# Order and queues of the opening loads in an attention, state-space and expert layer

## The chip, the cores and the metric

The kernel runs on one core of a Trainium2 chip. The core has five engines that run their own instruction streams: TensorE (PE, with its weight loads shown apart as PEld), VectorE (DVE), ScalarE (ACT), GpSimd (POOL) and SyncE (SP), which here only issues transfers. ScalarE issues transfers too. Sixteen DMA engines move the data. The metric is device time in microseconds; the time before is the median of three runs.

## The reference

One layer of a perceiver with 256 latents of width 512 and a context of 4096 rows of width 512, all in float32:

- x = x + attention(layernorm(x), context). 16 query heads and 4 key heads of width 128. Keys and values come both from the context (4096 keys, seen by all) and from the latents themselves (causal). Queries and keys are RMS-normed per head with a learned weight; queries and the latents' own keys are turned by rotary tables.
- x = x + state-space block(layernorm(x)).
- x = x + experts(layernorm(x)): 32 experts, the best 6 for each latent, and a shared one.

What matters here is only the start of the first part: layernorm(x), the first keys of the context (context times wk_ctx), the latents' own keys and queries, and the rotary tables, which are built once from cosines and sines (rope) and the norm weights (w_bc).

## The kernel before

**Tiling and stages.** The context is worked in eight chunks of 512 rows, each of four tiles of 128 rows. Chunk 0 is handled in the opening; chunks 1 to 7 are projected between the attention's steps. The latents are two row tiles of 128. A weight of 512 x 512 is held as four quarters of 128 rows (k = 0 to 3), so a projection of one tile is four matmuls in the code (eight instructions in the trace: a float32 matmul shows as two).

**The opening loads (L86 to L104, L132 to L138).** ScalarE's queue issues nw (the norm weights on one partition, for a flag), rope, w_bc (the norm weights copied to all partitions) and kw_col. rope has rows of 512 bytes, w_bc of 1 KB, kw_col of 4 bytes; the others have rows of 2 KB. SyncE's queue issues context tile 0 (`load_ctx0(0, 1)`), the keys' weights in three pieces (`load_wkc`: quarter 0, quarter 1, quarters 2 and 3), x, context tile 1, context tiles 2 and 3, and the values' weights wvc. Behind the branch on the flag (L1601 to L1608) SyncE issues wk, the four pieces of wq, wv and the next chunks. A transfer signals its landing on one of eight semaphores that are used in turn; a later transfer that takes the same one is issued only when the earlier one has landed.

**The opening work (L465 to L512).** TensorE's stream is: the keys of context tiles 0, 1 and 2 (ps_k, L309), the eight transposes of the normed latents (lnT, L212), the values of tile 0 (ps_v, L316), the transpose of the keys of tile 0 (kTp, L291), then the latents' own keys (ps_self, L479), which read the turned latents xT, with more transposes and queries behind it.

VectorE makes what these need: the layer norm of x (statistics at L201 and L203, then `power_half` with its small operation pv at L195, then xn at L206, one for each row tile), the rotary tables (`rope_table`, eight operations at L441 and L442 that read rope and w_bc, written into the first part of oacc), four small operations on w_bc (L555 to L559), pv for the keys' norms, and the two copies of the transposes into xT (L213). The power itself runs on GpSimd (L196). Behind the second power GpSimd makes three sums of the keys' and values' weights for a later stage (`weight_sums`, L330 to L332):

```python
with tc.issue_after(normed.ins):
    weight_sums(*sums)
```

where `normed` is the layer norm's last power.

**What sets the order.** Each engine runs its instructions in the order that a scheduler wrote at build time from the code, from costs and from what each instruction needs; `issue_after` adds a wish. The order in the code is thus not the order on VectorE: the table operations stand between the layer norm's. Transfers keep the order of the code on their queue.

Of the kernel before, what the change touches and what calls it, by code (L numbers as in the profile page):

```python
# [11 lines left out]
FP = mybir.dt.float32  # L12
# [7 lines left out]
P = 128  # L20
L = 256
NT = L // P
# [8 lines left out]
HD = 128  # L31
HALF = HD // 2
# [41 lines left out]
def perceiver_layer(ctx: ExitStack, tc: tile.TileContext, a: dict, out: bass.AP):  # L74
    nc = tc.nc
    V, S, G, TE = nc.vector, nc.scalar, nc.gpsimd, nc.tensor

    early = ctx.enter_context(tc.tile_pool(name="early", bufs=1))
    const = ctx.enter_context(tc.tile_pool(name="const", bufs=1))
# [10 lines left out]
    wkc, wvc = wkv[:, 0], wkv[:, 1]  # L90
# [1 line left out]


    load_ctx0 = lambda i, n: nc.sync.dma_start(ctx0[:, i:i + n], a["ctxT"][0, :, i:i + n])
    load_wkc = lambda k, n: nc.sync.dma_start(wkc[:, k:k + n, :],
                                              a["wk_ctx"][k * P:(k + n) * P, :].rearrange("(k p) n -> p k n", p=P))
    load_ctx0(0, 1)
    load_wkc(0, 1)
    load_wkc(1, 1)
    load_wkc(2, 2)  # L100
    nc.sync.dma_start(x_sb, a["x"].rearrange("(t p) d -> p t d", p=P))
    load_ctx0(1, 1)
    load_ctx0(2, 2)
    nc.sync.dma_start(wvc, a["wv_ctx"].rearrange("(k p) n -> p k n", p=P))  # L104

    nb = const.tile([1, 2], FP, name="nb")
    V.tensor_reduce(nb, nw, AX.X, ALU.max, apply_absolute_value=True)
# [20 lines left out]
    kd = [tc.dram_tile((CK // P, NKV, HD, P), FP, name=f"kd{c}") for c in range(NC)]  # L128
    blocks_d = [tc.dram_tile((REP, HD, P), FP, name=f"qd{i}") for i in range(NT * NH // REP)]
    sums_d = [tc.dram_tile((SH, P), FP, name=f"sums{t}") for t in range(NT)]  # L130

    rope = const.tile([P, NT, 2, HALF], FP, name="rope")  # L132
    S.dma_start(rope, a["rope"].rearrange("(t p) c h -> p t c h", p=P))
    w_bc = const.tile([P, 2, HD], FP, name="w_bc")
    S.dma_start(w_bc, a["norm_ws"].partition_broadcast(P))
    qw_bc, kw_bc = w_bc[:, 0, :], w_bc[:, 1, :]
    kw_col = const.tile([P, 1], FP, name="kw_col")
    S.dma_start(kw_col, a["norm_ws"][1, :].unsqueeze(1))  # L138

    def layer(ctx, bounded):  # L140
        small = ctx.enter_context(tc.tile_pool(name="small", bufs=4))
# [1512 lines left out]
```

## Time and profile before

| what | value |
|---|---|
| median of 3 runs | 992.71 us (991.9 to 994.02) |
| the profiled execution's own time | 989.35 us |
| its span in the profile | 987.6 us |
| TensorE busy | 968.4 us (98%) |
| VectorE busy | 497.8 us (50%) |
| ScalarE busy | 386.5 us (39%) |
| GpSimd busy | 206.0 us (21%) |
| moved | 125.91 MB, mean 127 GB/s |
| landing of rope, w_bc, kw_col after issue | 4.2, 5.6, 7.3 us |
| landing of the values' weights after issue at 6.08 | 9.5 us |

The profile shows one execution. A line of the timeline has the start, the duration of the group, the engine, the line of the code, the operation, what it writes and reads, how many instructions are merged, and in brackets the idle time before it and what ended it. In a table of stretches each engine's busy time and instruction count stand in one row, and the last two columns are the busy share of the DMA engines and GB/s. An engine's idle time matters only if TensorE, which is busy nearly throughout, comes to wait for it.

### The profile page before, as it was taken

Reading aid. Unit: us, or ns where it says so; the run is one execution under the profiler, and the core shown is the slowest. Engines: PE = TensorE matmul, PEld = TensorE weight load, DVE = VectorE, ACT = ScalarE, POOL = GpSimd, SP = SyncE. Lnnn points to the kernel's source line nnn. Section 1 sums busy time; section 2 is a strip of 40 time slices with the busy share of each in tenths; the row PEclk is TensorE's granted clock in tenths of the full one; section 3 lists DMA queues with packets and bytes.
Section 4 is the critical chain, followed back from the end, with each engine's and each line's share of the span. In section 5 each row is a group of like instructions: output and inputs, shape, how many; then the busy total and the mean of one; then the engine's idle time right before and its main releaser. Section 6 shows DMA issues by size and latency. Waiting matters only on the chain.

```text
span 987.6 us, 8901 instructions
## 1 busy us (share of the span) xinstructions
PE 968.4 (98%) x2742; PEld 456.0 (46%) x2742; DVE 497.8 (50%) x999; ACT 386.5 (39%) x851; POOL 206.0 (21%) x212
## 2 busy tenths in 40 slices
PE   7999999999999999999999999999999999999996
PEld 3444444444444444444444444444465655555442
DVE  4456555454453544544535545458496766422134
ACT  3645444443443434434434444353253731222210
POOL 4443001001100200200200100000013224554533
PEclk9999999999999999999999999999999999999999
DMA  9734142222313304304204112240046452999953
GB/s 319 235 74 118 56 117 94 45 39 111 85 21 128 85 2 147 82 4 150 66 20 124 56 35 46 83 128 1 0 157 199 184 193 106 353 351 352 397 221 117
DMA packets 131580, 125.91 MB, mean 127 GB/s; under 512 B 80225, under 2 KB 99586, under 8 KB 126274
## 3 DMA queue, kind: packets, MB, share of 16 engines
q1 hardware_dynamic: 119216, 77.96, 26.2%
q0 software_dynamic: 7984, 41.16, 11.2%
q10 hardware_dynamic: 4322, 6.11, 1.7%
q8 instruction: 24, 0.39, 0.2%
q14 instruction: 34, 0.28, 0.1%
HBM read 89.02 MB, written 36.19 MB: 127 GB/s over the span
## 4 chain that ended last, share of the span: by engine, by line
PE 94%; DMA 2%; DVE 1%; ACT 1%; POOL 1%; issue 1%; SPq 0%; POOLq 0%; DVEq 0%
PE scT L567 23%; PE oT L592 23%; PE ps_kv L364 17%; PE ps_egu L218 5%; PE ps_self L218 3%; PE ps_v L218 2%; PE ps_o L790 2%; PE ps_ye L1466 2%; PE ps_xbc L218 1%; PE ps_out L984 1%; PE ps_egu L1389 1%; PE ps_k L218 1%; PE ps_sgu L218 1%; PE total L1457 1%; PE xgTp L1370 1%; PE ps_ye L1469 1%
## 5 line engine op out<-in xcount | busy, mean ns | idle before, releaser
L583 DVE TENSOR_TENSOR lacc<-lacc,prT 128x512 f32<-128x512 f32 x256 | 182.6, 714 | 239.2 <-ACT prT L573 238.5
L573 ACT ACTIVATE prT<-scT,bq,rk 128x512 f32<-128x512 f32 x256 | 198.9, 777 | 253.9 <-PE scT L567 241.8
L567 PE MATMUL scT<-qT,kT 128*128 128x512 f32 x536 | 271.7, 593 | 0.0
L592 PE MATMUL oT<-prT,v 128*128 128x512 f32 x528 | 268.3, 592 | 0.0
L567 PEld LDWEIGHTS scT<-qT,kT 128*128 128x128 f32 x536 | 101.1, 190 | 124.8 <-issue 121.9
L592 PEld LDWEIGHTS oT<-prT,v 128*128 128x128 f32 x528 | 100.2, 190 | 125.8 <-issue 115.8
L196 POOL TENSOR_TENSOR rk<-pv,mhalf 128x4 f32<-128x4 f32 x32 | 32.3, 1010 | 369.2 <-DVE pv L195 369.2
L364 PE MATMUL ps_kv<-wkv,fast 128*128 128x512 f32 x112 | 53.4, 592 | 0.0
L254 ACT ACTIVATE sq<-kraw 128x128 f32<-128x128 f32 x128 | 35.6, 278 | 45.2 <-DVE kraw L382 43.2
L364 PE MATMUL ps_kv<-wkv,ctx 128*128 128x512 f32 x112 | 52.8, 592 | 0.0
L364 PE MATMUL ps_kv<-fast,fast 128*128 128x512 f32 x112 | 52.6, 592 | 0.0
L598 DVE TENSOR_TENSOR oacc<-oT,oacc 128x512 f32<-128x512 f32 x64 | 43.6, 681 | 0.0
L364 PEld LDWEIGHTS ps_kv<-wkv,fast 128*128 128x128 f32 x112 | 21.3, 190 | 26.8 <-issue 26.8
L364 PEld LDWEIGHTS ps_kv<-fast,fast 128*128 128x128 f32 x112 | 21.3, 190 | 26.8 <-issue 21.8
L364 PEld LDWEIGHTS ps_kv<-wkv,ctx 128*128 128x128 f32 x112 | 21.3, 190 | 26.8 <-issue 23.7
L358 POOL TENSOR_TENSOR fast<-ctx 128x512 f32<-128x512 f32 x7 | 9.4, 1337 | 113.1 <-PE ps_kv L364 94.2
L382 DVE TENSOR_TENSOR kraw<-ps_kv,fast 128x256 f32<-128x256 f32 x42 | 17.9, 426 | 28.2 <-PE ps_kv L364 28.2
L1441 DVE TENSOR_TENSOR hid<-si,ps_egu 128x128 f32<-128x128 f32 x18 | 5.2, 287 | 51.2 <-ACT si L1439 51.2
L790 PE MATMUL ps_o<-wo,qT 128*128 128x512 f32 x64 | 28.8, 592 | 0.0
L218 PE MATMUL ps_self<-wq,xT 128*128 128x512 f32 x64 | 28.1, 592 | 0.0
L603 DVE RECIPROCAL lacc<-ps_l 128x512 f32<-128x512 f32 x8 | 26.8, 3348 | 0.1
L364 PE MATMUL ps_kv<-fast,ctx 128*128 128x512 f32 x56 | 26.3, 592 | 0.0
(392 smaller groups left out, 1129.3 us busy)
## 6 DMA issues: line engine op xcount, KB each, us to landing
xg<-xn SPq DMA_DIRECT2D x6, 2560.0 KB, 9.7
ctx<-in_ctxT_dram SPq DMA_DIRECT2D x7, 1024.0 KB, 5.0
kd<-tr SPq DMA_DIRECT2D x112, 64.0 KB, 2.2
kT<-kd SPq DMA_DIRECT2D x28, 256.0 KB, 2.9
ye<-y_sb ACTq DMA_DIRECT2D x22, 256.0 KB, 8.4
wq<-in_wq_dram SPq DMA_DIRECT2D x4, 1024.0 KB, 14.2
wo<-in_wo_dram SPq DMA_DIRECT2D x4, 1024.0 KB, 7.7
w_in<-in_W_inT_dram SPq DMA_DIRECT2D x4, 1024.0 KB, 5.8
```

The lines of the kernel that those rows point to most:

```text
L196: return G.tensor_tensor(dst, v[:, :n], mhalf[:, :n], ALU.pow)
L218: TE.matmul(ps, lhs(k), rhs_of(k), start=(k == 0), stop=(k == KD - 1))
L254: S.activation(sq[:, h, :], raw[:, h, :], AF.Square, accum_out=ss[:, h:h + 1])
L364: TE.matmul(ps, lhs(k), rhs(k), start=(start and k == 0), stop=(k == 1), skip_group_check=True)
L567: scored.append(TE.matmul(sc, kT[:, g, i * P:(i + 1) * P], qT[:, t, heads4(g), :].rearrange("p h q -> p (h q)"), start=True, stop=True).ins)
L573: S.activation(pr, sc, AF.Exp, bias=shift, scale=SCALE if r is None else r[:, i, g:g + 1])
L583: V.tensor_tensor(la, la, pr, ALU.add)
L592: TE.matmul(outs[g, t], v[:, i, g * HD:(g + 1) * HD], pr, start=(n == 0), stop=last)
L598: V.tensor_tensor(ov, outs.pop((g, t)), ov, ALU.add)
L603: V.reciprocal(rl, ps)
L790: TE.matmul(m["ps_o", t], aT[:, t, h, :], wo[j][:, h % 4, :], start=(h == 0), stop=(h == NH - 1))
L1466: TE.matmul(ps[i], h[:, i, :], wd[i], start=True, stop=False)
```

## The change

The first quarter of the keys' weights is issued on ScalarE's queue, behind nw, instead of SyncE's. Context tile 1 stands ahead of x on SyncE's queue. rope, w_bc and kw_col go from ScalarE's queue to the end of SyncE's opening loads, behind the values' weights. No computation is changed.

```diff
-    load_wkc = lambda k, n: nc.sync.dma_start(wkc[:, k:k + n, :],
-                                              a["wk_ctx"][k * P:(k + n) * P, :].rearrange("(k p) n -> p k n", p=P))
+    load_wkc = lambda q, k, n: q.dma_start(wkc[:, k:k + n, :],
+                                           a["wk_ctx"][k * P:(k + n) * P, :].rearrange("(k p) n -> p k n", p=P))
     load_ctx0(0, 1)
-    load_wkc(0, 1)
-    load_wkc(1, 1)
-    load_wkc(2, 2)
+    load_wkc(nc.scalar, 0, 1)
+    load_wkc(nc.sync, 1, 1)
+    load_wkc(nc.sync, 2, 2)
+    load_ctx0(1, 1)
     nc.sync.dma_start(x_sb, a["x"].rearrange("(t p) d -> p t d", p=P))
-    load_ctx0(1, 1)
     load_ctx0(2, 2)
     nc.sync.dma_start(wvc, a["wv_ctx"].rearrange("(k p) n -> p k n", p=P))
+
+    rope = const.tile([P, NT, 2, HALF], FP, name="rope")
+    nc.sync.dma_start(rope, a["rope"].rearrange("(t p) c h -> p t c h", p=P))
+    w_bc = const.tile([P, 2, HD], FP, name="w_bc")
+    nc.sync.dma_start(w_bc, a["norm_ws"].partition_broadcast(P))
+    qw_bc, kw_bc = w_bc[:, 0, :], w_bc[:, 1, :]
+    kw_col = const.tile([P, 1], FP, name="kw_col")
+    nc.sync.dma_start(kw_col, a["norm_ws"][1, :].unsqueeze(1))
...
-    rope = const.tile([P, NT, 2, HALF], FP, name="rope")
-    S.dma_start(rope, a["rope"].rearrange("(t p) c h -> p t c h", p=P))
-    w_bc = const.tile([P, 2, HD], FP, name="w_bc")
-    S.dma_start(w_bc, a["norm_ws"].partition_broadcast(P))
-    qw_bc, kw_bc = w_bc[:, 0, :], w_bc[:, 1, :]
-    kw_col = const.tile([P, 1], FP, name="kw_col")
-    S.dma_start(kw_col, a["norm_ws"][1, :].unsqueeze(1))
```

In the built program TensorE's, ScalarE's and GpSimd's instructions stand in the same order as before. On VectorE the xn of row tile 0 now stands ahead of the second row tile's pv, with more of the table operations behind the second xn:

| position | before | after |
|---|---|---|
| after the statistics of both row tiles | L203, first L441 (waits for rope and w_bc), pv, L203, L442, pv | L203, first L441 (waits for rope and w_bc), pv, L203, L442, xn of tile 0, pv |
| then | L441, L442, L441, xn of tile 0, xn of tile 1 | L441, L442, xn of tile 1 |
| then | L442, L441, L442 | L441, L442, L441, L442 |
| then | four of L555 to L559, two pv, two xT copies | the same |

## The prediction

> **What bounds the kernel now.** I read the page's first part, then the busy time by stretches, then the timeline of each engine over the opening, since the change touches only transfers that are issued there.
>
> ```profile
> PE 968.4 (98%) x2742; PEld 456.0 (46%) x2742; DVE 497.8 (50%) x999; ACT 386.5 (39%) x851; POOL 206.0 (21%) x212
> ```
>
> The stretches (first column after the window is its length, then busy PE, PEld, DVE, ACT, POOL):
>
> ```profile
> 0.00:20.00 20.00, 14.60 (x34) 6.09 (x35) 8.40 (x27) 6.76 (x23) 6.84 (x14) 1.00 0.87 303
> 20.00:100.00 80.00, 79.97 (x205) 36.13 (x204) 43.66 (x76) 45.19 (x138) 35.43 (x31) 1.00 0.56 160
> 100.00:200.00 100.00, 100.00 (x235) 44.27 (x234) 49.05 (x82) 42.33 (x84) 9.10 (x8) 1.00 0.25 72
> ```
>
> TensorE has work without a break from about 10 us to 700 us. What the opening gains or loses for TensorE therefore passes one for one to the end; what it does to any other engine counts only where TensorE comes to wait for it. TensorE's own opening (start, duration):
>
> ```profile
> 5.29 13.52 PE L218 MATMUL ps_k<-wkv,ctx 128*128 128x512 f32 x24 [5.29 <-DMA wkv<-in_wk_ctx_dram]
> ...
> 18.64 1.04 PE L212 MATMUL lnT<-ident,xn 128*128 128x128 f32 x8
> ...
> 23.39 1.02 PE L218 MATMUL ps_self<-wk,xT 128*128 128x512 f32 x2
> ```
>
> It starts when the first quarter of the keys' weights lands, and 24 instructions take 13.5 us against 24 x 0.43 = 10.3 us at the later pitch. The last line is the first product that needs xT, the turned latents. Who makes xT:
>
> ```profile
> 11.06 1.29 DVE L201 BATCH_NORM_STATS2 bn<-x_sb 128x6 f32<-128x512 f32 x2 [8.20 <-DMA x_sb<-in_x_dram]
> ...
> 12.35 0.26 DVE L441 TENSOR_TENSOR oacc<-rope,w_bc 128x128 f32<-128x128 f32 x1
> 12.53 0.15 DVE L195 TENSOR_SCALAR pv<-mv 128x1 f32<-128x1 f32 x1
> ...
> 13.52 1.16 DVE L206 TENSOR_SCALAR xn<-x_sb,mv,rs 128x512 f32<-128x512 f32 x2
> ...
> 16.02 2.16 DVE L195 TENSOR_SCALAR pv<-ss 128x4 f32<-128x4 f32 x2
> 19.28 1.29 DVE L213 COPY xT<-lnT 128x512 f32<-128x512 f32 x2 [1.09 <-PE lnT L212]
> ```
>
> and GpSimd beside it, with the three weight sums:
>
> ```profile
> 12.83 1.27 POOL L196 TENSOR_TENSOR rs<-pv,mhalf 128x1 f32<-128x1 f32 x2 [10.77 <-DVE mv L203]
> 15.69 2.40 POOL L330 TENSOR_TENSOR oacc<-wkv 128x1024 f32<-128x1024 f32 x1 [1.59 <-DMA wkv<-in_wv_ctx_dram]
> 18.17 2.37 POOL L331 TENSOR_TENSOR oacc<-wkv,oacc 128x1024 f32<-128x1024 f32 x1
> 20.62 2.40 POOL L332 TENSOR_TENSOR oacc<-wkv,oacc 128x1024 f32<-128x1024 f32 x1
> ```
>
> The reader is to see that all eight rope-table operations (L441, L442) are over before the first weight sum begins, and that the tiny pv operation at 16.02 lasted until that sum ended at 18.09. The second xT copy ends at 20.57; TensorE asks for xT at 23.39: 2.8 us of slack, and 3.4 us for the first copy.
>
> **What the Trainium skill says.** "SBUF — State Buffer", Who interferes with whom: a VectorE instruction with two SBUF inputs contends with a GpSimd instruction that reads SBUF, and whichever starts first blocks the other for its whole duration. The trace agrees. Around 59 us, VectorE first, GpSimd below:
>
> ```profile
> 58.61 0.86 DVE L455 TENSOR_TENSOR lacc<-raw,oacc 128x256 f32<-128x256 f32 x1
> 59.40 1.48 DVE L456 TENSOR_TENSOR lacc<-raw,oacc 128x256 f32<-128x256 f32 x1
> ```
>
> ```profile
> 57.47 1.73 POOL L356 TENSOR_TENSOR fast<-ctx 128x512 f32<-128x512 f32 x1
> 59.28 1.33 POOL L357 TENSOR_TENSOR fast<-fast,ctx 128x512 f32<-128x512 f32 x1
> ```
>
> Both VectorE operations take 0.42 us undisturbed (at 28.8 and 29.1 us). Each ended 0.3 us after the GpSimd operation it met: one VectorE operation slips in between two GpSimd ones, not two. "DMA: Bandwidth & Descriptors", Queues, rings and completion order: each issuing engine has one ring on each of the 16 DMA engines, and a ring is consumed in order. In this trace SyncE's loads land in the order of issue. "TensorE: Matmul & The Clock Gate", What's actually happening: the array runs at half clock until it has been busy for a window of some 3.4 us. The trace agrees: starts 0.98 to 1.0 us apart from 5.29 to 9.3, 0.43 us from about 10.3.
>
> **The change, part by part.** (1) The first weight quarter moves from SyncE's to ScalarE's queue, where it is issued after nw at about 1.4 us, as rope is now; on SyncE it is issued at 1.26. No gain in issue time is certain. It shares the DMA engines with the second quarter. Bounds: its landing at 5.2 moves to between 4.5 and 6.1. (2) The remaining quarters, context tile 1, x and the rest lose the small packets ahead of them:
>
> ```profile
> 5.50:9.00 3.50, 3.50 (x4) 0.76 (x4) 0.00 (x0) 0.00 (x0) 0.00 (x0) 1.00 0.77 230
> 9.00:12.00 3.00, 2.89 (x6) 1.18 (x6) 0.94 (x2) 0.20 (x1) 0.00 (x0) 1.00 1.04 413
> ```
>
> (the last column is GB/s). While w_bc and kw_col trickled in, the engines moved 230 GB/s, afterwards about 400: 3.5 x (1 - 230/400) = 1.5 us lost, 0.2 us more from 4 to 5.5 (337 GB/s), and 262 KB of rope and w_bc are another 0.65 us: 2.4 us for the three. So TensorE's waits inside ps_k vanish. They are small, since the half-clock phase that covers them is not shortened by data that comes sooner: four starts 0.98 apart, one of 0.81 (9.46 to 10.27), nineteen of 0.43 make 12.9 us from the start instead of 13.35. With a start between 4.5 and 6.1, lnT is asked for between 17.4 and 19.0 instead of 18.64: +0.4 to -1.2 us, I take -0.4.
>
> (3) rope, w_bc and kw_col now stand on SyncE's queue behind the values' weights. Their issue slots cost nothing: each waits for one of the first three loads to land, by about 6 us, while the values' weights are still moving, and wk's issue behind them is at 7.71 now and is used only at 23.4. But VectorE's order in the built program is: statistics, first L441, which waits for rope and w_bc, and behind it the pv of the layer norm, xn of row tile 0, pv, L441, L442, xn of tile 1, then L441, L442, L441, L442, four bq operations, two pv of the keys, and only then the two xT copies. The wait on rope and w_bc is harmless now (5.6 and 7.4 us, x lands at 11.06). When do they land after? Ahead of them are 3.67 MB; 0.39 MB move by 4 us, the rest at 400 GB/s is done at 12.2; the values' weights now land when 0.43 MB more than what is ahead of them have moved, 1.1 us, so they land at 13.3 (15.6 now). rope and w_bc follow, between 0.65 us (bytes alone) and 2.4 us (all the small-packet cost); I take 1.4. Tw = 14.7, bounds 13.9 to 15.7.
>
> From Tw, by the durations above: pv +0.18, power +0.48, xn0 +1.17, second pv behind it +1.78, second power +2.08 to +2.72. xn1 starts at +2.77, ends at +3.3 (18.0): in time for lnT. But the values' weights have landed long before, so GpSimd goes straight from the power to the weight sums: L330 from +2.7 to +5.1, before the last four two-input table operations, which now meet it. The first gets in at +5.1, L331 runs to +7.8, the second gets in, L332 runs to +10.4, then the other two, four bq and two pv (1.3 us), and the first xT copy 0.7: xT at Tw + 12.4 = 27.1. TensorE, which would ask at 23.0 to 23.4, waits: 27.1 - 23.4 = +3.7 us against now. If two operations slip through each gap, xT comes at Tw + 11.0: +2.3. Late next is everything behind ps_self in TensorE's queue, and so the end. ScalarE's and GpSimd's later work has no due date before it. Sum: between the two with most weight on the first, +3.4 us, with (1) and (2) swallowed by the wait. On the profiled execution: span 987.6 to 991.0, its own time 989.35 to 992.8. The median shown, 992.71, is 3.4 above that execution, so 996.1 on the median.
>
> **The rivals.** *No stall, loads as meant* (the other side): xT is ready by the time TensorE asks for it. It decides at Tw = 23.4 - 12.4 = 11.0 or lower, or if the table operations get past the sums. Then only parts (1) and (2) count: -0.4, at the most -1.2: 991.5 to 992.3, no measurable change. For it: the DMA engines are busy from 4 us on, so everything is a bit sooner. Against it: Tw = 11.0 would need the remaining 3.5 MB moved in the 5.9 us from 4.0 to 9.9, at 600 GB/s. *Half clock gone as well*: a start at 4.2 (-1.1), the waits gone (-0.5) and two matmuls fewer at half clock (-1.1) give -2.7 us: 990.0; against it, nothing in the change makes TensorE busy earlier than the first quarter. *Late xn alone*: L441's wait delays the layer norm but the table operations are not blocked; lnT at Tw + 3.3 = 18.0 to 19.0, 0 to +0.4: 993. *Stall that cools the array*: a wait of 3.7 us can hold a whole idle window; then some four matmuls at 0.98 add 2 us: 998.1. For it, the size of the wait; against it, the same section calls the window free-running, and a whole one has to fit into the wait.
>
> **How the numbers follow.** Stall by the blocked table operations 0.70 (of it 0.06 with a cooled array), late xn or a short stall 0.10, loads as meant 0.14, half clock gone 0.06. The stall alone runs from Tw 13.9 with two per gap (+1.5) to 15.7 with one (+4.7), 994.2 to 997.4, 2 more with cooling. The range 991.9 to 998.0 leaves out the fastest case and most of the coolest. 0.2% is 2.0 us, about what a measurement of this kernel can tell from no change (the runs shown span 2.1). Slower by more than that: most of the stall's 0.70, less its lower end, 0.64; within: 0.28; faster: 0.08.
>
> **What would show it.** First L441 at 14 to 15.5 with x's statistics done several us before; L330 starting at the end of the second power; L441 and L442 behind xn stretched from 0.28 to over 2 us; xT copies at 25 to 27; TensorE's first wait between kTp and ps_self of 2 to 4 us, the rest of the trace shifted as a whole. Wrong if L441 starts before 11, or if the four table operations end before L330 begins.

## The result and the profile after

The changed kernel takes 997.5 us (median of 5 runs, 996.68 to 998.47) against 992.71 us: 1.0051 times as long, 95% interval 1.0036 to 1.0066. Beside a second set of runs of the kernel before it was 1.0050 (1.0036 to 1.0064), 994.59 against 990.51 us. It is slower by 0.5%, some 4.8 us. The kernel before took 992.71 us in the first set of runs and 989.7 to 990.5 us in the later ones, so times are compared only within a set. The profiled execution took 996.68 us, its span is 994.9 us.

Busy time by engine, then by stretches (length, busy PE, PEld, DVE, ACT, POOL, clock, DMA share, GB/s), of the changed kernel:

```profile
PE 968.1 (97%) x2742; PEld 456.7 (46%) x2742; DVE 500.9 (50%) x999; ACT 386.2 (39%) x851; POOL 205.9 (21%) x212
```

```profile
0.00:20.00 20.00, 13.08 (x28) 5.77 (x28) 4.98 (x15) 6.27 (x21) 3.96 (x13) 1.00 0.89 308
20.00:100.00 80.00, 76.33 (x198) 34.80 (x199) 46.14 (x83) 42.26 (x134) 38.55 (x32) 1.00 0.50 140
```

TensorE was busy for 14.60 and 79.97 us of these two stretches before, and for 13.08 and 76.33 now: 1.5 and 3.6 us less, so what was lost was lost early. TensorE's timeline over the opening says where (start, duration, idle time before it):

```profile
6.58 12.64 PE L218 MATMUL ps_k<-wkv,ctx 128*128 128x512 f32 x24 [6.58 <-DMA wkv<-in_wk_ctx_dram]
19.06 0.60 PE L212 MATMUL lnT<-ident,xn 128*128 128x128 f32 x4
21.40 0.66 PE L212 MATMUL lnT<-ident,xn 128*128 128x128 f32 x4 [1.74 <-DVE xn L206]
21.89 3.60 PE L218 MATMUL ps_v<-wkv,ctx 128*128 128x512 f32 x8
...
28.18 1.13 PE L218 MATMUL ps_self<-wk,xT 128*128 128x512 f32 x2 [2.25 <-DVE xT L213]
```

Subtract the starts before from these. The first matmul is 1.3 us late (6.58 against 5.29), the first transpose 0.4 (19.06 against 18.64): the early lateness is nearly made good. Then two waits that were not there before: for the second xn, and for xT. At ps_self, the first product that reads xT, the distance is 28.18 - 23.39 = 4.79 us. VectorE and GpSimd in the same stretch:

```profile
10.30 1.29 DVE L201 BATCH_NORM_STATS2 bn<-x_sb 128x6 f32<-128x512 f32 x2 [7.43 <-DMA x_sb<-in_x_dram]
...
16.14 0.29 DVE L441 TENSOR_TENSOR oacc<-rope,w_bc 128x128 f32<-128x128 f32 x1 [4.47 <-DMA w_bc<-in_norm_ws_dram]
...
17.26 0.55 DVE L206 TENSOR_SCALAR xn<-x_sb,mv,rs 128x512 f32<-128x512 f32 x1 [0.50 <-POOL rs L196]
...
18.71 2.63 DVE L206 TENSOR_SCALAR xn<-x_sb,mv,rs 128x512 f32<-128x512 f32 x1 [0.45 <-POOL rs L196]
21.26 2.48 DVE L441 TENSOR_TENSOR oacc<-rope,w_bc 128x128 f32<-128x128 f32 x1
23.67 0.28 DVE L442 SCALAR_TENSOR_TENSOR oacc<-rope,w_bc 128x128 f32<-128x128 f32 x1
23.87 2.48 DVE L441 TENSOR_TENSOR oacc<-rope,w_bc 128x128 f32<-128x128 f32 x1
...
27.44 1.28 DVE L213 COPY xT<-lnT 128x512 f32<-128x512 f32 x2
```

```profile
17.95 0.73 POOL L196 TENSOR_TENSOR rs<-pv,mhalf 128x1 f32<-128x1 f32 x1 [0.72 <-DVE pv L195]
18.65 2.41 POOL L330 TENSOR_TENSOR oacc<-wkv 128x1024 f32<-128x1024 f32 x1
21.14 2.46 POOL L331 TENSOR_TENSOR oacc<-wkv,oacc 128x1024 f32<-128x1024 f32 x1
23.67 2.53 POOL L332 TENSOR_TENSOR oacc<-wkv,oacc 128x1024 f32<-128x1024 f32 x1
```

x's statistics are done by 11.6 us, and VectorE stands still for 4.5 us until w_bc lands. Three VectorE operations then last 2.5 us instead of 0.28 or 0.55, and each ends 0.14 to 0.28 us after the weight sum beside which it ran: one for each sum. The xT copy, which began at 19.28 before, begins at 27.44.

In this execution the distance grew once more, from 5.0 to 6.9 us at 850 to 856 us, where ScalarE waited, and TensorE behind it. The first two lines are from the changed kernel's timelines of ScalarE and TensorE there, the third from ScalarE's in its second profile (experiment 9), where the distance did not grow:

```profile
855.82 0.33 ACT L1439 ACTIVATE si<-ps_egu 128x192 f32<-128x192 f32 x1 [2.57 <-remote]
856.52 0.33 PE L1448 MATMUL hidTp<-ident,hid 128*128 128x128 f32 x1 [1.80 <-DVE hid L1441]
```

```profile
854.67 0.33 ACT L1439 ACTIVATE si<-ps_egu 128x192 f32<-128x192 f32 x1 [2.19 <-PE ps_egu L218]
```

So it is not in every execution of the changed kernel; what that event is stays open. The two spans (994.9 and 987.6 us) differ by 7.3 us, the medians by 4.8. This event is one part of the difference; another is that the profiled execution of the kernel before, at 989.35 us, was 2.5 us faster than the fastest of its five runs (991.9).

### The profile page after: what moved, and what is told of

It is laid out like the page before. It is cut to its first block, busy times and chain, and to the rows that moved or that the text cites. A ratio compares the mean times of both kernels' runs of the same rounds, so it can differ in the third digit from the quotient of the medians.

```text
span 994.9 us, 8902 instructions
## 1 busy us (share of the span) xinstructions
PE 968.1 (97%) x2742; PEld 456.7 (46%) x2742; DVE 500.9 (50%) x999; ACT 386.2 (39%) x851; POOL 205.9 (21%) x212
## 4 chain that ended last, share of the span: by engine, by line
PE 91%; DVE 2%; DMA 2%; ACT 1%; POOL 1%; issue 1%; another core or an unknown queue 1%; ACTq 0%; POOLq 0%; DVEq 0%
PE oT L592 23%; PE scT L567 23%; PE ps_kv L364 17%; PE ps_egu L218 4%; PE ps_self L218 3%; PE ps_o L790 2%; PE ps_v L218 2%; PE ps_ye L1466 2%; PE ps_xbc L218 1%; PE ps_out L984 1%; PE ps_egu L1389 1%; PE ps_sgu L218 1%; PE total L1457 1%; PE xgTp L1370 1%; DMA w_bc<-in_norm_ws_dram 1%; PE ps_ye L1469 1%
```

## The experiments

Three theories were set against each other. A: w_bc comes late, so the last table operations and GpSimd's weight sums meet, and xT comes late. B: w_bc's lateness does it alone, through the layer norm that stands behind the first table operation. C: the first weight quarter's late landing is carried to the end. VectorE's order, which the scheduler wrote anew for the changed loads, is one more candidate; experiments 3 and 7 bear on it. Ratios are to runs of the kernel before beside them, with 95% intervals; distances are starts of TensorE's instructions minus those in the profile of the kernel before that was shown at the outset.

**1. The small loads back on ScalarE's queue** (w_bc and kw_col in the same way as rope, at the same place in the code).

```diff
-    nc.sync.dma_start(rope, ...)
+    S.dma_start(rope, ...)
```

> The changed kernel with rope, w_bc and kw_col back on ScalarE's queue, behind the first weight quarter; the rest of the change stays. Theory A (late w_bc puts the last table operations against the weight sums, and xT comes late): the tables are done before the sums start, TensorE does not wait for xN or xT, the end is at +0 to +0.6 us against the kernel before, some 993.0. Rival B (w_bc's lateness by itself, through the layer norm behind the first table operation): the same, since w_bc is early. Rival C (the first quarter's late landing, 1.3 us at TensorE's start, is carried to the end): +1.3 us, 994.0, TensorE's first matmul at 6 us or later and no later catching up.

989.86 us, ratio 0.9999 (0.9991 to 1.0008). TensorE's timeline:

```profile
5.92 13.46 PE L218 MATMUL ps_k<-wkv,ctx 128*128 128x512 f32 x24 [5.92 <-DMA wkv<-in_wk_ctx_dram]
...
23.96 1.02 PE L218 MATMUL ps_self<-wk,xT 128*128 128x512 f32 x2
```

No wait is marked at ps_self. The rest of the change is no measurable loss and no gain. C's 1.3 us would be 1.0013, outside the interval. But in this profile TensorE began only 0.6 us late, and at ps_self all of that was still there; 0.6 us would be 1.0006, inside the interval. So 1.3 us at the end is excluded, a carried 0.6 is not. The edit also changed VectorE's order in the built program: all eight table operations now stood ahead of the two xn, which were done at 16.44 us, still in time.

**2. The small loads moved, and nothing else** (in the kernel before, rope, w_bc and kw_col to behind the values' weights on SyncE's queue).

```diff
+    nc.sync.dma_start(rope, ...)
-    S.dma_start(rope, ...)
```

> The kernel before with only rope, w_bc and kw_col moved behind the values' weights on SyncE's queue. Theory A: the whole loss is there with this part alone: +4.3 to +5.0 us, 997.3; TensorE starts at 4.8 to 5.3 us and waits the longer for xT. Rival C: TensorE's start at 5.3 gives 1.3 us back: +3.5 us, 996.2.

993.6 us, ratio 1.0038 (1.0026 to 1.0051). TensorE's timeline:

```profile
5.38 12.81 PE L217 MATMUL ps_k<-wkv,ctx 128*128 128x512 f32 x24 [5.38 <-DMA wkv<-in_wk_ctx_dram]
18.03 0.60 PE L211 MATMUL lnT<-ident,xn 128*128 128x128 f32 x4
21.32 0.66 PE L211 MATMUL lnT<-ident,xn 128*128 128x128 f32 x4 [2.69 <-DVE xn L205]
...
28.11 1.13 PE L217 MATMUL ps_self<-wk,xT 128*128 128x512 f32 x2 [2.26 <-DVE xT L212]
```

Within the intervals, the whole loss is here (3.9 us by the medians): ps_self at 28.11, as with the full change, though TensorE began 1.2 us earlier. The earlier start only makes the wait for xn longer (2.69 instead of 1.74). The interval of the ratio holds both A's and C's figure; the trace decides for A.

**3. The weight sums later, w_bc as late as ever.** The powers are collected in a list, and the sums are put behind that of the second key tile:

```diff
-        with tc.issue_after(normed.ins):
+        with tc.issue_after(powers[3].ins):
             weight_sums(*sums)
```

> The changed kernel with GpSimd's three weight sums put behind the power for the second key tile, so that they cannot meet the table operations; w_bc is as late as in the changed kernel (16 us). Theory A: xn of tile 1 is ready at 19.3, xT at about 22, before TensorE asks for it at 23.8; only the late start's remainder is left: +0.4 us, 993.1. Rival B (late w_bc by itself delays the layer norm): TensorE still waits 2 us or more for xn or xT: 995.5 to 997.5.

990.04 us, ratio 1.0001 (0.9992 to 1.0009). VectorE's timeline, then TensorE's:

```profile
16.18 0.29 DVE L444 TENSOR_TENSOR oacc<-rope,w_bc 128x128 f32<-128x128 f32 x1 [4.81 <-DMA w_bc<-in_norm_ws_dram]
...
18.76 0.55 DVE L209 TENSOR_SCALAR xn<-x_sb,mv,rs 128x512 f32<-128x512 f32 x1 [0.45 <-POOL rs L198]
19.22 0.28 DVE L444 TENSOR_TENSOR oacc<-rope,w_bc 128x128 f32<-128x128 f32 x1
...
20.99 1.28 DVE L216 COPY xT<-lnT 128x512 f32<-128x512 f32 x2
```

```profile
23.73 1.02 PE L221 MATMUL ps_self<-wk,xT 128*128 128x512 f32 x2
```

This decides between A and B. VectorE waits for w_bc as long as before, until 16.18 us, but every operation up to the xT copies has its short duration again, xT is copied from 20.99 instead of 27.44, and TensorE does not wait. Late w_bc alone costs nothing that can be measured. VectorE's order is here that of the changed kernel, so that order alone is not the cause either.

The stretches of this run also say something about when w_bc lands (length, busy PE, PEld, DVE, ACT, POOL, clock, DMA share, GB/s):

```profile
5.50:9.00 3.50, 2.21 (x3) 1.17 (x4) 0.00 (x0) 0.00 (x0) 0.00 (x0) 1.00 1.05 400
9.00:12.00 3.00, 3.00 (x6) 1.10 (x5) 1.37 (x3) 0.00 (x0) 0.00 (x0) 1.00 1.04 395
12.00:14.40 2.40, 2.40 (x7) 1.14 (x6) 0.00 (x0) 2.07 (x3) 0.00 (x0) 1.00 1.04 224
```

Until 12 us the loads moved at the forecast 400 GB/s, and w_bc was late all the same; the slow stretch comes after.

**4. The table operations later, loads and sums as in the change.** They, and the four small ones on w_bc, are put behind the last xT copy:

```diff
-        rope_table(tab_k, kw_bc)
-        rope_table(tab_q, qw_bc)
+        with tc.issue_after(turned.ins):
+            rope_table(tab_k, kw_bc)
+            rope_table(tab_q, qw_bc)
```

> The changed kernel with the eight table operations and the four small ones on w_bc put behind the xT copies on VectorE; loads and sums stay. Theory A: xn is ready at about 13, xT at 20.5, no wait of TensorE between the keys and the queries; +0.4 us, 993.1. Rival B: the same. Rival C: the late start costs all of its 1.3 us: 994.0.

989.71 us, ratio 1.0000 (0.9991 to 1.0008). ps_self began at 24.92 without a wait. TensorE's first matmul was as late as 7.32 us in this execution, 2.0 us late, and 1.5 us of that was still there at ps_self. The xT copies began at 21.55, a microsecond later than expected: the transposes that they copy began only at 20.17, and two small operations ahead of the copies now met the sums. VectorE's timeline, then GpSimd's:

```profile
17.20 2.00 DVE L195 TENSOR_SCALAR pv<-ss 128x4 f32<-128x4 f32 x1 [3.27 <-ACT sq L254]
19.41 2.22 DVE L195 TENSOR_SCALAR pv<-ss 128x4 f32<-128x4 f32 x1 [0.21 <-ACT sq L254]
21.55 1.27 DVE L213 COPY xT<-lnT 128x512 f32<-128x512 f32 x2
```

```profile
14.36 2.37 POOL L330 TENSOR_TENSOR oacc<-wkv 128x1024 f32<-128x1024 f32 x1 [1.01 <-DMA wkv<-in_wv_ctx_dram]
```

The last line shows when the values' weights land with the changed loads, which the changed kernel's own profile doesn't show: the sum waits for them until 14.36 us.

**5. As 4, with the first quarter on SyncE's queue again.**

```diff
-    load_wkc(nc.scalar, 0, 1)
+    load_wkc(nc.sync, 0, 1)
```

> As e4 (tables behind the xT copies), and the first weight quarter back on SyncE's queue, behind context tile 0. Theory A: TensorE starts at 5.0 to 5.3 us without the small packets in its way and never waits in the opening: -0.5 us against the kernel before, 0.9995 of its time. If the late start in e1, e3 and e4 came from the chip and not from the queue, TensorE starts at 6 us or later here too.

988.94 us against 989.75: ratio 0.9989 (0.9982 to 0.9995), the only version whose interval lies below the kernel before. TensorE began at 5.73 and did not wait. The profiled execution doesn't show a gain: its first seven matmuls ran at half pace (0.85 to 0.99 us from one start to the next, 0.43 later), and ps_self was at 23.89. This version differs from experiment 4 in the first quarter's queue alone. Their intervals overlap narrowly (0.9982 to 0.9995, 0.9991 to 1.0008), so a cost of up to about 1 us for that quarter's place on ScalarE's queue, once the stall is gone, is neither shown nor excluded.

**6. The change, with only the first quarter on SyncE's queue again** (the same edit in the changed kernel).

> The changed kernel with only the first weight quarter back on SyncE's queue. Theory A: the start moves from 6.6 to about 5.2 us, and the wait for xT swallows it: ps_self at 28.1 us, the end at +4.3 to +4.8 us, ratio 1.0045 as for the whole change. Rival C (the start is carried to the end): 1.3 us less than the whole change, +3.4 us, ratio 1.0034.

993.95 us, ratio 1.0042 (1.0026 to 1.0057). TensorE's timeline:

```profile
5.08 12.06 PE L218 MATMUL ps_k<-wkv,ctx 128*128 128x512 f32 x24 [5.08 <-DMA wkv<-in_wk_ctx_dram]
...
20.79 0.66 PE L212 MATMUL lnT<-ident,xn 128*128 128x128 f32 x4 [2.86 <-DVE xn L206]
21.29 5.29 PE L218 MATMUL ps_v<-wkv,ctx 128*128 128x512 f32 x8
...
27.57 1.12 PE L218 MATMUL ps_self<-wk,xT 128*128 128x512 f32 x2 [0.56 <-DVE xT L213]
```

A start that is 1.5 us earlier than in the changed kernel is swallowed: w_bc was 0.6 us earlier in this execution (first table operation at 15.55), and ps_self is earlier by the same 0.6. The eight ps_v took 5.29 us instead of 3.60: after the wait of 2.86 us four of the matmuls ran at half clock (the granted clock was 0.63 from 20.7 to 25 us), and even that was swallowed by the wait for xT.

**7. kw_col back on ScalarE's queue.**

```diff
-    nc.sync.dma_start(kw_col, ...)
+    S.dma_start(kw_col, ...)
```

> The changed kernel with only kw_col (rows of 4 bytes) back on ScalarE's queue; a look at when w_bc lands. If kw_col's packets, which some DMA engines reach while others still have w_bc to do, keep w_bc from landing: first table operation at 15.0 us or earlier instead of 16.1. If not: 15.8 to 16.2.

The first table operation was at 15.53 us, between the two expectations. Since it was at 15.51 to 16.18 in four runs with kw_col in place (experiments 2, 3, 6 and 9), this tells nothing about kw_col. The edit did more than move one load: VectorE's order in the built program changed too, to one nearer that of the kernel before, with both xn together at 16.65. ps_self came 11.1 us after the first table operation instead of 12.0, so in this one run the other order was worth about 1 us, and the stall was there all the same. TensorE's timeline has something else:

```profile
26.65 2.07 PE L218 MATMUL ps_self<-wk,xT 128*128 128x512 f32 x2 [2.27 <-DVE xT L213]
28.51 0.85 PE L291 MATMUL kTp<-ident,kraw 128*128 128x128 f32 x3
```

Two matmuls lasted 2.07 us instead of 1.13, and the distance went from 3.3 us at ps_self to 4.8: the array had gone back to half clock (0.59 granted from 26.6 to 30.5 us). 994.75 us, one run.

**8. w_bc from 128 different rows.**

```diff
-    nc.sync.dma_start(w_bc, a["norm_ws"].partition_broadcast(P))
+    nc.sync.dma_start(w_bc, a["rope"].rearrange("(p t) c h -> p t (c h)", t=2))
```

> The changed kernel with w_bc filled from 128 different rows of 1 KB (the rotary tables' memory) instead of one row of 1 KB read 128 times; the tables are then wrong, and nothing else is left out. If reading the same row over and over makes w_bc slow: first table operation at 15.2 us or earlier instead of 16.1, xT and the end earlier by as much. If it is the size of the packets alone: 15.8 to 16.2.

VectorE's timeline:

```profile
15.16 0.29 DVE L441 TENSOR_TENSOR oacc<-rope,w_bc 128x128 f32<-128x128 f32 x1 [3.76 <-DMA w_bc<-in_rope_dram]
```

1.0 us earlier than in the changed kernel's profile (0.35 us earlier than in any run with the single row), and ps_self 1.06 us earlier, at 27.12: 993.11 us, one run. That reading one row 128 times is slower than reading 128 rows agrees with this; one run doesn't show it, with 0.67 us between the runs that kept the single row.

**9. The change once more.** (No edit.)

> The changed kernel once more, beside the same runs of the kernel before as e10. Theory A: TensorE reaches ps_self at 28 us instead of 23.4, and this distance, 4.2 to 4.8 us, stays to the end: ratio 1.0045. The further 2 us by which the first profile of the changed kernel was late from 850 us on (ScalarE waiting there) belong to that execution: the distance at the end is again the one at ps_self. If they belong to the change, they are here again, and the distance ends near 7.

994.59 us, ratio 1.0050 (1.0036 to 1.0064). TensorE's timeline:

```profile
27.56 1.45 PE L218 MATMUL ps_self<-wk,xT 128*128 128x512 f32 x2 [2.26 <-DVE xT L213]
28.80 1.06 PE L291 MATMUL kTp<-ident,kraw 128*128 128x128 f32 x4
29.65 1.92 PE L218 MATMUL ps_self<-wk,xT 128*128 128x512 f32 x2
```

ps_self is 4.17 us late; the half clock that follows the wait (0.59 granted from 27.5 to 31.5 us) adds 1.6 us (5.7 from 31.4 us on), and after that the distance moves by no more than 0.4 us to the end. The 2 us at 850 us are not there.

**10. The kernel before, with the table operations later** (edit of experiment 4, loads as before).

> The kernel before with its own loads, and the table operations and the four small ones on w_bc behind the xT copies, as in e5. If e5's gain of 0.1% comes from the loads: no change, ratio 0.9997 to 1.0003, TensorE never waits for xT in either. If it comes from VectorE's order: ratio 0.9989 as e5.

989.65 us against 990.51, ratio 0.9994 (0.9986 to 1.0003). This lies between the two expectations: whether the 0.1% of experiment 5 comes from the loads or from VectorE's order stays open.

## Why the prediction was right, and where it was off

It foretold slower, by 3.4 us, through a stall at xT; measured were 4.8, and 997.5 us is near the top of the range given (991.9 to 998.0). The sum is of the distance at ps_self, which was 4.79 in the one profile. That the medians of the first set differ by just as much is in part chance: in the later sets the loss was 3.9 to 4.2 us by the medians (experiments 2, 6 and 9).

- **The mechanism** (part 3) holds at every link: the wait of the first L441 for w_bc (4.5 us), the sums that start as the second power ends (18.65), the stretched operations, the wait between kTp and ps_self (2.25 us, forecast 2 to 4). Experiment 2 has the loss with part 3 alone, experiment 3 has none although w_bc is as late, experiment 4 has none with the table operations out of the way.
- **The step that was off is Tw**, taken as 14.7 us with bounds of 13.9 and 15.7: it was 16.14 in the changed kernel's profile, and 15.51 to 16.18 in four repeats (experiments 2, 3, 6 and 9). Of the sum's shortfall of 1.4 us (4.8 against 3.4), this 16.14 - 14.7 = 1.4 is all. I had let the queue move 400 GB/s from 4 us on, and it moved 373 and 377 from 5.5 to 12 us in the changed kernel. That cannot be the main reason: in experiment 3 it moved 400 and 395 there, and w_bc was as late. The term that was too small is the cost of the small rows, which I had worked out from their old place, 1.4 us (at most 2.4) from 13.3 on; 16.14 is 2.8 later than that. The rate fell already from 12 us on (224 GB/s up to 14.4 in experiment 3), and the values' weights, forecast for 13.3, landed at 14.36 in experiment 4. In experiments 7 (kw_col elsewhere) and 8 (w_bc from 128 rows) the stretch from 12 to 14.4 us moved 356 and 362 GB/s, against 210 to 322 in the seven profiles with both loads as in the change; these are one run each and only suggest that both take part.
- **From Tw to xT** I had 12.4 us with one operation for each gap between the sums, 11.0 with two. To the end of the first copy it was 28.12 - 16.14 = 12.0. But the distribution was another: I let xn of tile 1 finish beside the first sum ("in time for lnT"), and it was the first operation to be blocked (2.63 us). So the rival of the late xn was real as well, and added a wait of 1.7 us ahead of lnT. It doesn't add to the end, since the wait for xT swallows it. After the second sum, two table operations went through. The total held because in both accounts three operations are blocked, one by each sum; which three, I had wrong in part.
- **The first quarter** was to land between 4.5 and 6.1 us. With it on ScalarE's queue TensorE began at 6.58, 5.92, 6.79, 7.32, 6.07, 6.83 and 7.13 us in seven profiles, with it on SyncE's at 5.29, 5.38, 5.73, 5.08 and 5.63 in five. This edit works against its purpose by some 1.2 us at TensorE's start. In the changed kernel's profile 0.4 us of its lateness was left at lnT, where I had expected -0.4; in the six others it was between -0.6 and 1.5. Without the stall the cost at the end is at most about 0.9 us (the intervals of experiments 1, 3 and 4 end at 1.0008 and 1.0009); with it, experiment 6 shows that the stall hides it.
- **The cooled array** was given a small part of the stall's chance. It came in three of six profiles with the stall (experiments 6, 7 and 9, not in the changed kernel's first profile, nor in experiments 2 and 8), and added 1.5 us in two of them; in experiment 6 the later wait hid it. It was a likely companion, and too lightly weighed.
- **The other side**, no stall, was right about its size: with the stall taken away (experiments 1, 3 and 4) the changed loads are worth nothing measurable. Its condition, Tw below 11 or the table operations past the sums, is what experiments 3 and 4 made true in the second form.

The runs settle the cause, with the loss at xT. They put Tw's lateness mainly on the small rows and not on the rate before them; they do not settle how it divides among rope, w_bc's single row and kw_col.

## What to carry to other kernels

A load that is moved back in a queue is not free because its consumer has slack: look in the built order at what stands behind that consumer on its engine, and at what the delay will make it run beside. Here 4.8 us of waiting were harmless by themselves (experiment 3). What cost was that xn and some table operations were pushed into the time of three long GpSimd operations, and that three of them each waited for one of these to end (2.5 us instead of 0.28 or 0.55). In this kernel the order on either engine cured it with the late loads in place (experiments 3 and 4).

## What the runs showed of the hardware

- The Trainium skill, "SBUF — State Buffer" (Who interferes with whom), has a VectorE operation contend with GpSimd when it has two SBUF inputs or runs in a 2-port mode, which it says tensor_scalar operations can enter. xn, a tensor_scalar with one tensor input and two per-partition scalars, was blocked by a GpSimd sum: 2.63 us against 0.55 (changed kernel), and again in experiments 2, 6, 7, 8 and 9. Whether it was in such a mode, no run shows. Beside GpSimd's power of a 128x1 operand the same xn ran in 0.54 us (kernel before).
- The Trainium skill, "TensorE: Matmul & The Clock Gate" (What's actually happening), has the array cool after an idle window of about 3.4 us. Here waits of 2.26 and 2.27 us at xT (experiments 9 and 7) were followed by matmuls at half clock, with 0.59 granted over the next 4 us, while waits of 2.25 and 2.26 us (changed kernel, experiment 2) were not, with 1.00 granted. The idle time before the cooling was shorter than the page's figure.
- The second transfer on ScalarE's queue, issued at 1.38 us, landed at 5.9 to 7.3 us by TensorE's start; the same 256 KB issued on SyncE's queue at 1.26 us landed at 5.1 to 5.7. Here the second queue was slower than the place behind one transfer on the first, with the next quarter moving beside it; why, no run shows.
